# Softmax weights two steps closer to their maxima, and the maxima's transpose one step earlier

## The chip, the cores and the metric

The kernel runs on one core of a Trainium2 chip. The metric is the device time of one execution in microseconds (us). The time before is 3572.62 us, the median of 3 runs (3572.36 to 3573.77).

## The reference

One layer over 4096 tokens of width 256: attention with 16 heads of width 16, then a gated feed-forward network of width 1024, each with a residual and a layer norm.

```python
proj = quant4(x) @ ternary_weight(Wqkv_w).T + Wqkv_b      # q, k, v all from one projection
q = proj.reshape(B, N, h, dk).transpose(0, 2, 1, 3)
k = proj.reshape(B, h, N, dk);  v = proj.reshape(B, h, N, dk)
q, k = rotary(q, N), rotary(k, N)
ql, kl = q @ U, k @ U
att = einsum('bhnr,bhmr->bhnm', ql, kl) / sqrt(dk)
y = softmax(att, axis=-1) @ v
x = layernorm(x + quant4(y) @ ternary_weight(Wo_w).T)
h = silu(tlin(x, w1)) * tlin(x, w2);  h = gelu(tlin(h, h1));  h = gelu(tlin(h, h2))
x = layernorm(x + tlin(h, w3))
```

The softmax is the large part: 16 heads of 4096 by 4096 scores, each needing the maximum of its row before the exponential.

## The kernel before

**Units and steps.** Attention is cut into 64 units (`NU`). A unit is a pair of heads and a block of 512 queries; unit u has pair u // 8 and query block u % 8. A unit takes 32 steps (`NKT`), and one list of steps s runs through all units: step s belongs to unit s // 32. The order on every engine is the order in which this loop issues work; nothing rearranges it. Work other than the three streams below is put in a table `todo` with `at(step, f)`, and a step first runs its entries in the order in which they were put there:

```python
for s in range(NKT * NU + LAG + AVLAG + 4):
    while todo.get(s):
        todo[s].pop(0)()
    if s < NKT * NU and s % 2:
        largest(s)
    if 0 <= s - LAG < NKT * NU:
        weights(s - LAG)
    if s < NKT * NU and not s % 2:
        largest(s)
```

So an odd step has its table entries, then maxima, then weights; an even step has its entries, then weights, then maxima.

**Three streams.** `largest(s)` (L660, L671) makes scores with TensorE, 128 queries by 512 keys for each of the two heads, and VectorE reduces each to its maximum. In steps before `LAG` both heads' scores lie in one PSUM tile of the pool `ps_sc` and one reduction (L668) covers both. From then on they take two of the three single-bank buffers of `ps_1`. `weights(s - LAG)` (L709, L717) makes the scores again with the keys on the partitions: a first matmul subtracts the maxima (operand `m_rows`), a second adds the scores, ScalarE takes the exponential. `values` (L731), every second step and `AVLAG` = 4 steps behind the weights, multiplies them with v.

**The maxima's way.** At the last step of unit u VectorE folds the partial maxima into `m` (L676). One step after the unit's end, at 32 (u + 1) + 1, `largest_parts(u)` splits them into two float32r parts, the high one by ScalarE (L683), the low one by GpSimd (L684). Two steps later `largest_rows(u)` has VectorE transpose them into `m_turned` (L690), and the SyncE queue stores them to `m_dram` (L695) and, when that has landed, loads them twice as rows, one half for each head, into `m_rows` (L698). The unit's first `weights` step, 32 u + `LAG`, reads `m_rows`.

**What else hangs on `LAG`.** `end` = 32 u + `LAG` + 35 is the step of `finish(u)` (ScalarE copies the unit's result, L749). From it eight VectorE transposes `turn` (L763, at `end` + 2 to `end` + 16), the `gather` (four stores `y_raw`, L771, and a load `y`, L781, at `end` + 18), `add_strips` (GpSimd, L792, at `end` + 26) and `divide` (VectorE L801, GpSimd L803, a store L809, at `end` + 28).

**What does not.** In units 0 to 7 the projections of the eight token blocks run beside the attention, at fixed steps. For block b, counted from step 32 (b - 1): the queue's loads of `keys` (L545) at 28 for b of 3 and more, TensorE's product with them `times_g` (L553, with a VectorE subtraction L556) at 34 and 36, stores of `k_dram` (L592) at 37, and for the next block a scale round trip `ma_dram` (L469), `scale` (L471) and the table `cs_q` (L339) at -2. The keys `kT` of the next pair (L600, four loads of 512 KB) come at steps 40, 48, 56 and 64 from the start of the unit with query block 2. The first front of the feed-forward part, `integers` (L131 to L154 on VectorE), is put at step 2048 + 2, its transposes (L160) at 2048 + 8. The feed-forward stage follows the loop.

Of the kernel before, what the change touches and what calls it, by code (L numbers as in the profile page):

```python
# [27 lines left out]
NKT = N // P  # L28
# [9 lines left out]
def attn_ffn_kernel(  # L38
# [262 lines left out]
    with ExitStack() as actx:  # L301
# [295 lines left out]
        def load_keys(pair, kT, j, d):  # L597

            row = 64 * j + 32 * d
            nc.sync.dma_start(  # L600
                out=kT[row : row + 32].bitcast(F32),
                in_=k_dram[pair][j].rearrange("i e c n -> (i e) (c n)"),
            )

        def load_queries(u):

            pair, qb = divmod(u, NQB)
            qTs[u] = qpool.tile([P, QB], F32R, name="qT", bufs=3)
            for j in range(2):
                for i in range(2):  # L610
                    row = 64 * j + 2 * DK * i
                    nc.sync.dma_start(
                        out=qTs[u][row : row + 2 * DK, :].bitcast(F32),
                        in_=q_dram[qb][2 * pair + j, i].unsqueeze(0).broadcast_to([2, DK, QB]),
                    )
# [17 lines left out]
            project(held, sgn_qkv, bank1, i0, evacuate)  # L633

        NU = (H // 2) * NQB
        LAG = NKT + 8
        AVLAG = 4
        kTs, qTs, mxs, ms, avs, probs = {}, {}, {}, {}, {}, {}
        yas, yts, y4s, ys = {}, {}, {}, {}
# [2 lines left out]
        def at(step, f):  # L642
            todo.setdefault(step, []).append(f)

        def largest(s):
# [6 lines left out]

            both = ps_sc.tile([P, 2, QB], F32, name="sc") if s < LAG else None
            ps = [
# [26 lines left out]
        def largest_parts(u):  # L681
            parts, m = m_parts[:, 0], ms.pop(u)
            nc.scalar.copy(parts[:, :, 0, :], m)  # L683
            nc.gpsimd.tensor_tensor(  # L684
                parts[:, :, 1, :], m, parts[:, :, 0, :].bitcast(F32), ALU.subtract
            )

        def largest_rows(u):

            nc.vector.transpose(  # L690
                m_turned, m_parts.bitcast(F32).rearrange("p a j k t -> p (a j k t)")
            )

            rows = m_dram[u % 2]
            nc.sync.dma_start(out=rows.rearrange("r (b c) -> b r c", b=4), in_=m_turned)  # L695
            rows = rows[: 4 * BT].rearrange("(j k t) c -> j k (t c)", j=2, k=2)
            for j in range(2):
                nc.sync.dma_start(  # L698
                    out=m_rows[u % 2][64 * j : 64 * j + 2, :].bitcast(F32), in_=rows[j]
                )  # L700
# [19 lines left out]
        def values(s):  # L720

            u, kt = divmod(s, NKT)
            pair = u // NQB
            if kt == 0:
                avs[u] = ps_av.tile([P, QB], F32, name="av")
            for j in range(2):
                for k in range(2):
                    c, a = divmod(kt + k, 2)
                    strip = 32 * (2 * j + k)

                    nc.tensor.matmul(  # L731
                        avs[u][strip : strip + 32, :],
                        lhsT=v_all[
                            :, 2 * (2 * pair + j) + a, c * (DK + 1) : c * (DK + 1) + 32
                        ],
                        rhs=probs[s + k][:, j, :],
                        start=(kt == 0),
                        stop=(kt == NKT - 2),
                    )
            del probs[s], probs[s + 1]  # L740

        def finish(u):


            if u < NU - 1:
                yas[u] = qpool.tile([P, QB], F32, name="ya", bufs=1)
            else:
                yas[u] = last_unit[:, :QB]
            nc.scalar.copy(yas[u], avs.pop(u))  # L749
            if u < NU - 1:  # L750
                yts[u] = qpool.tile([P, QB], F32, name="yt", bufs=1)
# [8 lines left out]
        def turn(u, i):  # L760


            nc.vector.transpose(yts[u][:, ts(i, 64)], yas[u][:, ts(i, 64)])  # L763

        def gather(u):

            del yas[u]
            raw = y_raw[u % 2]
            yt = yts.pop(u).rearrange("p (b e) -> p b e", e=32)
            for strip in range(4):  # L770
                nc.sync.dma_start(  # L771
                    out=raw.rearrange("(b q) s e -> s q b e", q=32)[strip],
                    in_=yt[32 * strip : 32 * strip + 32],
                )
            if u < NU - 1:
                y4s[u] = qpool.tile([P, BT, 2, 2, 32], F32, name="y4", bufs=1)
            else:
                y4s[u] = last_unit[:, QB:].rearrange(
                    "p (t j k e) -> p t j k e", t=BT, j=2, k=2
                )  # L780
            nc.sync.dma_start(  # L781
                out=y4s[u].rearrange("p t j k e -> p t (j k e)"),
                in_=raw.rearrange("(t p) s e -> p t (s e)", p=P),
            )

        def add_strips(u):
            y4 = y4s.pop(u)
            if u < NU - 1:
                ys[u] = qpool.tile([P, BT, 2, DK + 1], F32, name="y", bufs=1)
            else:  # L790
                ys[u] = y4[:, :, :, 0, : DK + 1]
            nc.gpsimd.tensor_tensor(  # L792
                ys[u], y4[:, :, :, 0, : DK + 1], y4[:, :, :, 1, : DK + 1], ALU.add
            )

        def divide(u):

            pair, qb = divmod(u, NQB)
            y = ys.pop(u)
            den = stat.tile([P, BT, 2], F32, name="den")  # L800
            nc.vector.reciprocal(den, y[:, :, :, DK])  # L801
            yu = stat.tile([P, BT, 2, DK], F32, name="yu", bufs=2)
            nc.gpsimd.tensor_tensor(  # L803
                yu,
                y[:, :, :, :DK],
                den.unsqueeze(3).broadcast_to([P, BT, 2, DK]),
                ALU.mult,
            )
            nc.sync.dma_start(  # L809
                out=y_dram[qb].rearrange("(t p) d -> p t d", p=P)[  # L810
                    :, :, pair * 32 : (pair + 1) * 32
                ],
                in_=yu.rearrange("p t j e -> p t (j e)"),
            )
# [33 lines left out]
        with tc.manual_schedule():  # L848
# [85 lines left out]
            for u in range(NU):  # L934
                pair, qb = divmod(u, NQB)
                if qb == 2 and pair + 1 < H // 2:

                    def start_keys(pair=pair, u=u):
                        kTs[pair + 1] = kpool.tile([P, N], F32R, name="kT")
                        for i in range(4):  # L940
                            at(
                                NKT * u + 40 + 8 * i,
                                lambda i=i: load_keys(pair + 1, kTs[pair + 1], i // 2, i % 2),
                            )

                    at(NKT * u + 8, start_keys)
                if u:
                    at(NKT * (u - 1) + (25 if u < 3 else 23 if u < NQB else 14), lambda u=u: load_queries(u))
                base = NKT * u + LAG
                for kt in range(0, NKT, 2):  # L950
                    at(base + kt + 1 + AVLAG, lambda s=NKT * u + kt: values(s))
                at(NKT * (u + 1) + 1, lambda u=u: largest_parts(u))
                at(NKT * (u + 1) + 3, lambda u=u: largest_rows(u))
                end = base + NKT + AVLAG - 1
                at(end, lambda u=u: finish(u))
                if u == NU - 1:
                    left += [turn_last, lambda u=u: add_strips(u), lambda u=u: divide(u)]
                    continue
                for i in range(8):
                    at(end + 2 + 2 * i, lambda u=u, i=i: turn(u, i))  # L960
                at(end + 18, lambda u=u: gather(u))
                at(end + 26, lambda u=u: add_strips(u))
                at(end + 28, lambda u=u: divide(u))
# [33 lines left out]
            at(last - 60, start_front)  # L997
# [9 lines that stand above are left out]
# [259 lines left out]
```

## Time and profile before

| what | value |
|---|---|
| median of 3 runs | 3572.62 us |
| the profiled execution | 3571.62 us, span 3569.5 us |
| granted TensorE clock, mean | 0.994 |
| attention at full rate, unit 54 (2400.0 to 2443.2) | 43.20 us for 32 steps, PE busy 43.20, DVE 41.34, ACT 31.58 |
| maxima alone, ahead of the first weights (39 to 80 us) | DVE busy 38.04 of 41.00, PE 30.42 |
| weights and values alone, behind the last maxima (2855.4 to 2893 us) | PE busy 37.42 of 37.60, ACT 30.98, DVE 9.06 |
| chain that ended last | PE 97%, DVE 2%, DMA 1%, POOL 1% |
| DMA | mean 40 GB/s; q1, the SyncE queue's, 13.9% of 16 engines |

Times are microseconds from the start of the span of one profiled execution. PE is TensorE's matmuls, PEld its weight loads, DVE VectorE, ACT ScalarE, POOL GpSimd, SPq the SyncE queue that issues DMAs. Matmul ends are modelled, so a full PE row means that matmuls follow each other, and starts are what is to be read. A time behind a row in brackets is idle time of the engine before it, with what ended it.

### The profile page before, as it was taken

The numbers are of one execution on the slowest core, as the hardware profiler recorded it, in microseconds if no ns is written. First come the engines' busy times: TensorE is split into PE (matmuls) and PEld (weight loads), VectorE is DVE, ScalarE is ACT, GpSimd is POOL, SyncE is SP. The second block draws the span as 40 slices with busy tenths as digits, with TensorE's granted clock in tenths as the row PEclk, the third lists the DMA queues.
The fourth block names the chain that finished last, engine by engine and source line by source line (L and its number), as shares of the span: only waits on it lengthen the run. The fifth ranks groups of instructions, "written<-read, shape, count | busy, mean of one in ns | idle before, by whom it ended". The sixth has DMA issues, their size and how long they took to land.

```text
span 3569.5 us, 61116 instructions
## 1 busy us (share of the span) xinstructions
PE 3527.7 (99%) x23855; PEld 1983.6 (56%) x23855; DVE 3042.7 (85%) x5575; ACT 2337.1 (65%) x2713; POOL 437.1 (12%) x530
## 2 busy tenths in 40 slices
PE   6999999999999999999999999999999999999999
PEld 3444555555555555555555555555555458888887
DVE  8888999999999999999999999999999935555544
ACT  2677777777777777777777777777777753333333
POOL 5766200000000000000000000000000010000000
PEclk8999999999999999999999999999999999999999
DMA  3343212111211121111111111111121030000000
GB/s 102 89 121 89 55 27 50 27 27 30 51 29 27 27 50 27 28 37 42 27 27 44 33 27 27 44 27 24 47 68 33 24 93 1 25 30 18 18 7 13
DMA packets 267826, 141.88 MB, mean 40 GB/s; under 512 B 184584, under 2 KB 243848, under 8 KB 266632
## 3 DMA queue, kind: packets, MB, share of 16 engines
q1 hardware_dynamic: 263704, 126.35, 13.9%
q0 software_dynamic: 3824, 11.54, 1.0%
q8 instruction: 189, 3.10, 0.4%
q14 instruction: 109, 0.89, 0.1%
HBM read 91.57 MB, written 42.07 MB: 37 GB/s over the span
## 4 chain that ended last, share of the span: by engine, by line
PE 97%; DVE 2%; DMA 1%; POOL 1%; ACT 0%; issue 0%; SPq 0%; POOLq 0%; ACTq 0%
PE av L731 28%; PE sc L709 27%; PE ps L660 22%; PE ps_mm L1045 18%; DVE mx L668 1%; PE ps L553 1%; PE ps L483 0%; PE ps L172 0%; PE ps_mm L172 0%; PE ps_mm L290 0%; PE ps_mm L1087 0%; DMA qT<-q_dram 0%; DMA ma_dram<-ma_turned 0%; PE sc L660 0%; PE ps L160 0%
## 5 line engine op out<-in xcount | busy, mean ns | idle before, releaser
L671 DVE TENSOR_REDUCE mx<-ps 128x1 f32<-128x512 f32 x4016 | 2501.4, 683 | 137.4 <-PE ps L660 82.2
L717 ACT ACTIVATE pr<-sc 128x1024 f32<-128x1024 f32 x2048 | 1994.8, 1021 | 738.1 <-PE sc L709 736.4
L731 PE MATMUL av<-pr,v_all 128*32 128x512 f32 x8192 | 1092.1, 605 | 0.0
L660 PEld LDWEIGHTS ps<-kT,qT 64*128 64x128 f32 x4016 | 546.1, 183 | 949.7 <-DVE mx L671 812.0
L660 PE MATMUL ps<-kT,qT 64*128 64x512 f32 x4016 | 1015.4, 469 | 2.5 <-DMA qT<-q_dram 2.1
L709 PE MATMUL sc<-m_rows,minus 64*128 64x512 f32 x4096 | 823.1, 396 | 0.5 <-DVE mx L668 0.3
L709 PE MATMUL sc<-qT,kT 64*128 64x512 f32 x4096 | 815.5, 392 | 0.0
L709 PEld LDWEIGHTS sc<-m_rows,minus 64*128 64x128 f32 x4096 | 390.9, 185 | 95.0 <-ACT pr L717 36.4
L709 PEld LDWEIGHTS sc<-qT,kT 64*128 64x128 f32 x4096 | 390.6, 185 | 85.7
L731 PEld LDWEIGHTS av<-pr,v_all 128*32 128x32 f32 x8192 | 161.4, 108 | 257.4 <-issue 255.8
L1075 ACT ACTIVATE gate<-ps_mm,sc_hs 128x512 f32<-128x512 f32 x128 | 88.2, 689 | 288.5 <-PE ps_mm L1045 248.4
L283 DVE CAST h<-gate 128x512 fp32r<-128x512 f32 x128 | 54.3, 424 | 223.6 <-ACT gate L1075 223.4
L684 POOL TENSOR_TENSOR m_parts<-m,m_parts 128x8 fp32r<-128x8 f32 x64 | 13.0, 203 | 1809.6 <-ACT m_parts L683 1809.2
L285 DVE TENSOR_TENSOR h<-gate,h 128x512 fp32r<-128x512 f32 x192 | 132.3, 689 | 5.1
L1045 PE MATMUL ps_mm<-h,h1a 128*128 128x512 f32 x512 | 128.9, 394 | 0.0
L1067 DVE SCALAR_TENSOR_TENSOR gate<-ps_mm,sc_s,gate 128x512 f32<-128x512 f32 x64 | 47.9, 749 | 94.1 <-ACT gate L1065 73.9
L1045 PE MATMUL ps_mm<-h,h2a 128*128 128x512 f32 x512 | 127.1, 390 | 0.0
L1045 PE MATMUL ps_mm<-h,h1b 128*128 128x512 f32 x512 | 126.5, 389 | 0.0
L1045 PE MATMUL ps_mm<-h,h2b 128*128 128x512 f32 x512 | 126.5, 389 | 0.0
L763 DVE STREAM_TRANSPOSE yt<-ya 128x64 f32<-128x64 f32 x504 | 116.9, 233 | 0.0
L1045 PEld LDWEIGHTS ps_mm<-h,h1b 128*128 128x128 f32 x512 | 96.1, 188 | 20.1
L1045 PEld LDWEIGHTS ps_mm<-h,h2b 128*128 128x128 f32 x512 | 96.1, 188 | 19.9
(199 smaller groups left out, 1721.1 us busy)
## 6 DMA issues: line engine op xcount, KB each, us to landing
y_raw<-yt SPq DMA_DIRECT2D x256, 64.0 KB
qT<-q_dram SPq DMA_DIRECT2D x252, 64.0 KB
y<-y_raw SPq DMA_DIRECT2D x63, 256.0 KB
kT<-k_dram SPq DMA_DIRECT2D x28, 512.0 KB
xs<-in_x SPq DMA_DIRECT2D x16, 512.0 KB
q_dram<-qk SPq DMA_DIRECT2D x32, 256.0 KB
k_dram<-qk SPq DMA_DIRECT2D x56, 128.0 KB
cs_q<-in_csq SPq DMA_DIRECT2D x8, 512.0 KB
```

The costliest lines, as they stand in the source:

```text
L283: eng(dst[:, k, 0, :], g)
L285: nc.vector.tensor_tensor(dst[:, k, 1, :], g, dst[:, k, 0, :].bitcast(F32), ALU.subtract)
L553: nc.tensor.matmul(ps, lhsT=gmat, rhs=held["keys"][:, x], start=True, stop=True)
L660: nc.tensor.matmul(ps[j], lhsT=qTs[u][rows, ts(qt, P)], rhs=kTs[u // NQB][rows, ts(ck, 512)], start=True, stop=True,)
L671: nc.vector.tensor_reduce(mxs[u][:, qt, j, ck : ck + 1], ps[j], AX.X, ALU.max)
L709: nc.tensor.matmul(ps[:, j, :], lhsT=minus[rows, :] if first else kTs[u // NQB][rows, ts(kt, P)], rhs=m_rows[u % 2][rows, :] if first else ...
L717: nc.scalar.activation(pr, ps, AF.Exp)
L731: nc.tensor.matmul(avs[u][strip : strip + 32, :], lhsT=v_all[:, 2 * (2 * pair + j) + a, c * (DK + 1) : c * (DK + 1) + 32], rhs=probs[s + k ...
L763: nc.vector.transpose(yts[u][:, ts(i, 64)], yas[u][:, ts(i, 64)])
L1045: nc.tensor.matmul(ps, lhsT=sb[:, ks, ts(o, P)] if split else wo[:, k, :], rhs=src[:, k, i, :], start=(k == 0 and i == 0), stop=(k == n - ...
L1067: nc.vector.scalar_tensor_tensor(g, pb, scales["s2"][:, o : o + 1], gate, ALU.mult, ALU.mult)
L1075: nc.scalar.activation(g, ps, AF.Gelu, scale=scales[sc][:, o : o + 1])
```

## The change

`LAG` goes from 40 to 38: every weights and values step, and with them `finish`, the turns, the gather, the addition and the division, stand two steps earlier against the maxima; the loop has two steps fewer. `largest_rows` goes from three steps behind the unit's end to two, an even step instead of an odd one.

```diff
         NU = (H // 2) * NQB
-        LAG = NKT + 8
+        LAG = NKT + 6
         AVLAG = 4
...
                 at(NKT * (u + 1) + 1, lambda u=u: largest_parts(u))
-                at(NKT * (u + 1) + 3, lambda u=u: largest_rows(u))
+                at(NKT * (u + 1) + 2, lambda u=u: largest_rows(u))
                 end = base + NKT + AVLAG - 1
```

## Prediction

> **What bounds the kernel now.** I read the page's shares and its chain first, then the timeline of one boundary between units, then the SyncE queue around the early units, then the two ends of the attention. The page says that TensorE sets the time:
>
> ```profile
> PE 3527.7 (99%) x23855; PEld 1983.6 (56%) x23855; DVE 3042.7 (85%) x5575; ACT 2337.1 (65%) x2713; POOL 437.1 (12%) x530
> ...
> PE 97%; DVE 2%; DMA 1%; POOL 1%; ACT 0%; issue 0%; SPq 0%; POOLq 0%; ACTq 0%
> ```
>
> The timeline around the end of unit 21 shows one period of two steps and the way of the maxima:
>
> ```profile
> 1027.82 0.20 POOL L684 TENSOR_TENSOR m_parts<-m,m_parts 128x8 fp32r<-128x8 f32 x1 [34.67 <-ACT m_parts L683]
> ...
> 1029.06 1.06 PE L731 MATMUL av<-pr,v_all 128*32 128x512 f32 x8
> ...
> 1030.29 0.20 DVE L690 STREAM_TRANSPOSE m_turned<-m_parts 128x32 f32<-128x32 f32 x1
> ...
> 1030.52 0.57 SPq L695 DMA_DIRECT2D m_dram<-m_turned  x1
> ...
> 1031.76 1.07 PE L731 MATMUL av<-pr,v_all 128*32 128x512 f32 x8
> ...
> 1032.50 0.54 SPq L698 DMA_DIRECT2D m_rows<-m_dram  x2
> ...
> 1033.32 0.19 PEld L709 LDWEIGHTS sc<-m_rows,minus 64*128 64x128 f32 x2
> 1033.55 0.39 PE L709 MATMUL sc<-m_rows,minus 64*128 64x512 f32 x2
> ...
> 1036.26 0.40 PE L709 MATMUL sc<-m_rows,minus 64*128 64x512 f32 x2
> ```
>
> The values come at 1029.06 and again at 1031.76: 2.70 us for two steps, 43.20 for the 32 of a unit, with TensorE matmuls back to back. VectorE has four reductions in a period, 0.60 apart, so about 0.2 is free. The first matmul that reads unit 21's `m_rows` is the last row, at 1036.26. So in mid-kernel neither the place of the transpose nor the lag is on the path, as long as `m_rows` lands in time; what the change can give lies at the two ends, and what it can cost lies in the slack of that landing.
>
> **The two ends.** After the change two maxima steps fewer stand alone at the start, two weights steps fewer at the end, and two more are combined, with the same matmuls in all. At the start a step alone takes VectorE's L668 (four in 4.61 us from 79.12, and 1.17 apart in other rows): two are 2.34. The combined pair costs 2.70. Start: 2.70 - 2.34 = +0.36. At the end the values follow each other at 2865.31, 2867.42, 2869.78, 2871.91 and 2874.27, so a pair of steps takes 2.11 to 2.36: -2.24. In the last unit the weights wait for their rows, and the transpose stands behind the 5 us of `integers`:
>
> ```profile
> 2852.84 0.20 DVE L690 STREAM_TRANSPOSE m_turned<-m_parts 128x32 f32<-128x32 f32 x1
> ...
> 2856.52 0.77 PE L709 MATMUL sc<-m_rows,minus 64*128 64x512 f32 x2 [0.18 <-DMA m_rows<-m_dram]
> ```
>
> Both are now put at step 2050, and the transpose was put there first, so VectorE runs it ahead: it starts when POOL's L684 is done, near 2849.2, and the 0.18 goes. `integers` then waits for it, from 2847.84 to about 2849.4; its end moves from 2852.92 to 2854.5, under the transposes that need it (L160, 2855.72). Without that cover of 1.2 us the remainder would be lost on TensorE. Ends together: 0.36 - 2.24 - 0.18 = -2.06.
>
> **The landing in mid-kernel.** The weights come two steps earlier, 2.70 us; the first reader moves from 1036.26 to 1033.55, its weight load to 1033.32. The transpose passes only the last two reductions ahead of it, 2 x 0.60: from 1030.29 to 1029.09. L684 ended at 1028.02, so VectorE doesn't wait there; behind L690 on VectorE stand the reductions of one step. They start 0.20 later, as they do behind L676 (0.22, in the same kind of place at 1026.51), after which the next values still came in a period of 2.70: cost nothing. The trip from transpose to readable rows: the semaphore records have the second `m_rows` transfer landed at 1034.12, 3.83 after the transpose, and the last unit's pair of rows, 2852.84 to 2856.52 and a wait, agrees within 0.15. New landing 1029.09 + 3.83 = 1032.92, 0.40 before the weight load and 0.63 before the matmul; over units 8 to 62 the same sum leaves 0.25 to 0.42. I take no stall. Finish, turns and `divide` keep their odd steps, hence the free 0.2 us of a period; GpSimd's L792 and the store L809 come two steps earlier, behind the maxima's way as before. Unit 7 is tight by the same sum (second row landed 4.63 after the transpose, five small scale loads ahead of it): between 0 and 0.4, taken as 0, because these loads follow the gather and leave earlier too.
>
> Here the Trainium skill speaks against the change. Its page "DMA: Bandwidth & Descriptors", section "Anatomy of one DMA", gives each transfer a fixed cost of about 2.0 us (written for GpSimd's queue). The rows have 1.98 for the store (1030.52 to the next issue at 1032.50) and 1.33 for the second load (1032.79 to 1034.12). By the page's figure twice, an estimate, the rows land at 1033.6 and each unit loses about 0.3 us, 16 us in all.
>
> **The early units, where the queue order changes.** The gather moves from step 29 to step 27 of a unit, and in the windows of units 2 to 6 that puts it ahead of the `keys` loads (step 28). In four of these five this is covered: in unit 2 the keys would go out near 169.8 instead of 164.8 and are read at 177.43. Unit 3 has the large `kT` loads too:
>
> ```profile
> 213.18 0.41 SPq L600 DMA_DIRECT2D kT<-k_dram  x1
> 214.38 3.05 SPq L545 DMA_DIRECT2D keys<-rot  x4
> 218.50 5.29 SPq L771 DMA_DIRECT2D y_raw<-yt  x4
> 226.14 0.38 SPq L781 DMA_DIRECT2D y<-y_raw  x1
> ...
> 230.20 0.59 SPq L600 DMA_DIRECT2D kT<-k_dram  x1
> 230.85 0.58 SPq L695 DMA_DIRECT2D m_dram<-m_turned  x1
> 237.00 0.54 SPq L698 DMA_DIRECT2D m_rows<-m_dram  x2
> ```
>
> `kT` is not through before 223.4 by the semaphores, and the load `y` waits for the four stores behind it. With the gather first, `y` goes near 224.7, the keys at 225.1 to 227.5, the second landing near 227.8: `times_g`, at 227.03 before, waits about 0.8. The queue then reaches `m_dram` 0.76 later, 231.6, and as it needs 6.15 us behind `cs_q` and `kT`, the rows land at 238.61 + 0.76 = 239.4. Their reader, the matmul of 235.62, stands at 236.4 by then: a stall of 3.0. Unit 3 costs 3.8. The low bound is 0: the stores leave 2.7 earlier, and if `y` does too, the queue drains earlier and nothing waits. I take 3.8 because `kT`, not the turn, ended the stores' wait in this trace. Unit 1: GpSimd's L684 ends at 131.00, and the transpose would now stand at 130.22, so VectorE waits up to 0.8, with `times_g` on TensorE behind it. Bounds 0 and 0.8; I take 0.8.
>
> **Sum.** -2.06 + 3.8 + 0.8 = +2.5 on the profiled execution's 3571.62, so 3574.1; the median lies 1.0 above that execution: 3575.1.
>
> **Rivals.** (A) The sum above, 3575. (B) The queue drains in time in units 1 and 3: only the ends are left, 3572.6 - 2.1 = 3570.5. For it: everything that the gather issues is ready 2.7 earlier. (C) The rows come late in every unit. It decides from the point where the trip takes over 4.23 us (3.83 + 0.40). An excess of 0.3 over units 7 to 62 is 56 x 0.3 = 17: about 3592, the side of slower. For it: the margin is a tenth of the trip. Against it: 55 trips in this trace lie within 0.2 us of each other. (D) The stall in unit 3 halves the TensorE clock:
>
> ```profile
> 122.40:129.20 6.80, 6.45 (x19) 2.12 (x21) 1.98 (x3) 1.23 (x2) 6.46 (x8) 0.50 0.47 144
> ```
>
> In this stretch the granted clock is 0.50 for 6.80 us, after TensorE had waited for `qT` and buffers from 120.6 on; half of that, 3.4, would come on top of (A): 3578.5. The page "TensorE: Matmul & The Clock Gate", Part 1, has the clock halve after an idle window of about 3.4 us, so a stall of 3.0 is on its edge. Clock windows may fall otherwise around the first weights too (81.4 to 88.2 at 0.50): 1 us either way, in the range.
>
> **How the numbers follow.** A 0.50, B 0.30, D 0.10, C 0.08, 0.02 for what I don't see. A measurement of this kernel can tell about 0.2% (7.1 us) from no change. A and B lie inside it, D inside but near its edge (3579.8), C beyond. Faster 0.03, within 0.83, slower 0.14. The range 3569.5 to 3581 takes in A, B with its microsecond, and D; C is left out.
>
> **What would show it.** Right: period 2.70 and m_rows rows without a bracket in units 8 to 62; the `keys` rows behind the `y` row in unit 3, with a bracket "DMA" before L553 or L709 there; one pair less of values behind the last maxima; L690 ahead of L131 at 2849. Wrong: brackets "DMA m_rows" in many units (C), or unit 3 without any (B).

## The result, and the profile after

The changed kernel takes 3577.38 us (median of 22 runs, 3574.97 to 3580.48); the kernel before took 3572.07 in the runs beside it (22 runs, 3570.57 to 3573.93). The ratio is 1.0015, 95% interval 1.0009 to 1.0022: 5.3 us slower, inside the predicted range and within 0.2%. The profiled execution of the changed kernel took 3575.91 us with a span of 3573.7, against 3571.62 and 3569.5 before. A second profiled execution of each kernel, both on one chip, gave spans of 3574.3 and 3568.5.

The page's shares and its chain, after:

```profile
PE 3527.8 (99%) x23848; PEld 1986.6 (56%) x23855; DVE 3044.7 (85%) x5577; ACT 2336.8 (65%) x2713; POOL 436.6 (12%) x530
...
PE 94%; DVE 2%; POOL 2%; issue 1%; DMA 1%; ACT 0%; SPq 0%; POOLq 0%; ACTq 0%; DVEq 0%
```

TensorE still sets the time. The timeline of the changed kernel around the end of unit 21 answers to the one shown of before:

```profile
1031.79 0.20 POOL L684 TENSOR_TENSOR m_parts<-m,m_parts 128x8 fp32r<-128x8 f32 x1 [37.37 <-ACT m_parts L683]
...
1033.04 1.07 PE L731 MATMUL av<-pr,v_all 128*32 128x512 f32 x8
1033.07 0.20 DVE L690 STREAM_TRANSPOSE m_turned<-m_parts 128x32 f32<-128x32 f32 x1
...
1033.30 0.58 SPq L695 DMA_DIRECT2D m_dram<-m_turned  x1
...
1035.29 0.54 SPq L698 DMA_DIRECT2D m_rows<-m_dram  x2
...
1035.74 1.07 PE L731 MATMUL av<-pr,v_all 128*32 128x512 f32 x8
...
1037.31 0.19 PEld L709 LDWEIGHTS sc<-m_rows,minus 64*128 64x128 f32 x2
```

The values are 2.70 apart. The store takes 1.99 to the next issue. The second load of rows landed at 1037.04 by the semaphores, 3.97 after the transpose, and the weight load at 1037.31 has no bracket: the margin is 0.27 us. By the semaphores the margin lies between 0.18 and 0.42 in 52 of the units 8 to 62; units 29 and 61, with trips of 4.25 and 4.46, have none left. Of the units 7 to 62 only unit 56 waits.

To see where the 4 to 6 us are, I took the start of the values' matmuls (L731) at equal steps in both kernels; the difference after minus before, taken stretch by stretch, is the loss of that stretch. The last column is the second pair of executions. The loss of steps 269 to 1805, where it is spread over all units, is called the slow loss below.

| stretch | predicted | first pair | second pair |
|---|---|---|---|
| first weights and unit 1 (to step 77) | +1.16 | +0.94 | +1.17 |
| steps 77 to 109 | 0 | +0.09 | +0.12 |
| steps 109 to 141, with unit 3's first weights | +3.8 | +2.31 | +4.10 |
| steps 141 to 269 | 0 | +0.43 | +0.32 |
| steps 269 to 1805, most of the 43.2 us units | 0 | +1.18 | -0.19 |
| steps 1805 to 1837, with unit 56's first weights | 0 | +1.15 | +1.09 |
| steps 1837 to 2029 | 0 | +0.24 | +0.20 |
| steps 2029 to 2053, the last maxima | 0 | +0.82 | +0.83 |
| step 2053 to the last values | -2.42 | -2.61 | -2.54 |
| behind the last values | 0 | -0.39 | +0.68 |
| sum | +2.5 | +4.2 | +5.8 |

**Unit 1**, timeline of the changed kernel:

```profile
129.47 0.20 POOL L684 TENSOR_TENSOR m_parts<-m,m_parts 128x8 fp32r<-128x8 f32 x1
...
129.71 0.21 DVE L690 STREAM_TRANSPOSE m_turned<-m_parts 128x32 f32<-128x32 f32 x1 [1.95 <-POOL m_parts L684]
...
130.55 0.50 PE L660 MATMUL ps<-kT,qT 64*128 64x512 f32 x1 [1.82 <-DVE mx L671]
```

VectorE waits 1.95 us for GpSimd's low parts, and TensorE 1.82 behind it; in the second execution it is 3.60 and 3.47. From 119 to 132 us TensorE is idle for 2.15 and 1.96 us in the two executions of before, and for 3.48 and 3.59 in the two of the changed kernel.

**Unit 3**, timeline of the changed kernel:

```profile
224.19 0.38 SPq L781 DMA_DIRECT2D y<-y_raw  x1
...
224.66 2.46 SPq L545 DMA_DIRECT2D keys<-rot  x4
...
228.56 1.10 PE L553 MATMUL ps<-keys,gmat 128*128 128x512 f32 x2 [0.38 <-DMA keys<-rot]
...
230.49 0.60 SPq L600 DMA_DIRECT2D kT<-k_dram  x1
...
231.19 0.57 SPq L695 DMA_DIRECT2D m_dram<-m_turned  x1
...
237.13 0.54 SPq L698 DMA_DIRECT2D m_rows<-m_dram  x2
...
238.63 0.84 PE L709 MATMUL sc<-m_rows,minus 64*128 64x512 f32 x2 [1.35 <-DMA m_rows<-m_dram]
```

The `keys` now stand behind `y`, as predicted (225.1 to 227.5 there, 224.66 to 227.12 here), and the product with them waits. The store of the maxima goes out right behind a `kT` load of 512 KB and is through 5.94 us later; the weights wait 1.35 us for the rows.

**Unit 56**, timeline of the changed kernel:

```profile
2552.14 0.57 POOL L194 DMA_DIRECT2D w<-in_w2T  x1
...
2553.05 0.57 SPq L695 DMA_DIRECT2D m_dram<-m_turned  x1
...
2556.75 0.54 SPq L698 DMA_DIRECT2D m_rows<-m_dram  x2
...
2558.20 0.70 PE L709 MATMUL sc<-m_rows,minus 64*128 64x512 f32 x2 [0.77 <-DMA m_rows<-m_dram]
```

GpSimd issues a 512 KB load of feed-forward weights 0.9 us ahead of the store; the store takes 3.70 and not 1.99, and the margin is gone. Before, the load stood 2.5 us ahead of the store. Timeline of the kernel before:

```profile
2546.80 0.57 POOL L194 DMA_DIRECT2D w<-in_w2T  x1
...
2549.28 0.57 SPq L695 DMA_DIRECT2D m_dram<-m_turned  x1
...
2551.27 0.54 SPq L698 DMA_DIRECT2D m_rows<-m_dram  x2
```

**The last maxima**, timeline of the changed kernel:

```profile
2855.59 0.21 DVE L690 STREAM_TRANSPOSE m_turned<-m_parts 128x32 f32<-128x32 f32 x1 [1.32 <-POOL m_parts L684]
2855.72 1.18 DVE L131 TENSOR_REDUCE most<-yb 128x4 f32<-128x1024 f32 x1
...
2856.93 0.16 DVE L137 TENSOR_REDUCE ma<-most 128x4 f32<-128x8 f32 x1
...
2857.13 0.20 ACT L141 ACTIVATE ma<-ma 128x4 f32<-128x4 f32 x1 [0.72 <-DVE ma L137]
...
2858.30 0.50 PE L709 MATMUL sc<-m_rows,minus 64*128 64x512 f32 x2 [0.66 <-ACT pr L717]
```

The transpose runs ahead of `integers`, as predicted. But `integers` has an instruction on ScalarE, L141, between two exponentials. It waits 0.72 for VectorE, the next exponential waits behind it, and the weights wait 0.66 for that.

### The profile page after: what moved, and what is told of

It is laid out like the page before. It is cut to its first block, busy times and chain, and to the rows that moved or that the text cites. A ratio compares the mean times of both kernels' runs of the same rounds, so it can differ in the third digit from the quotient of the medians.

```text
span 3573.7 us, 61125 instructions
## 1 busy us (share of the span) xinstructions
PE 3527.8 (99%) x23848; PEld 1986.6 (56%) x23855; DVE 3044.7 (85%) x5577; ACT 2336.8 (65%) x2713; POOL 436.6 (12%) x530
## 4 chain that ended last, share of the span: by engine, by line
PE 94%; DVE 2%; POOL 2%; issue 1%; DMA 1%; ACT 0%; SPq 0%; POOLq 0%; ACTq 0%; DVEq 0%
PE av L731 27%; PE sc L709 26%; PE ps L660 21%; PE ps_mm L1045 18%; DVE mx L668 1%; PE ps L553 1%; DVE mx L671 0%; DMA m_dram<-m_turned 0%; PE ps L483 0%; PE ps_mm L172 0%; PE ps_mm L290 0%; PE ps_mm L1087 0%; PE ps L172 0%; ACT pr L717 0%; PE ps L580 0%
## 5 line engine op out<-in xcount | busy, mean ns | idle before, releaser
L731 PE MATMUL av<-pr,v_all 128*32 128x512 f32 x8192 | 1091.9, 605 | 0.1
L731 PEld LDWEIGHTS av<-pr,v_all 128*32 128x32 f32 x8192 | 161.8, 108 | 258.0 <-issue 256.0
L684 POOL TENSOR_TENSOR m_parts<-m,m_parts 128x8 fp32r<-128x8 f32 x64 | 12.9, 202 | 1961.9 <-ACT m_parts L683 1961.5
```

Source lines behind the costliest of these rows:

```text
L731: nc.tensor.matmul(avs[u][strip : strip + 32, :], lhsT=v_all[:, 2 * (2 * pair + j) + a, c * (DK + 1) : c * (DK + 1) + 32], rhs=probs[s + k ...
```

## The experiments

Theory: the changed kernel's 2.5 us and more are rows that come late where something large lies on the queue or the DMA engines, plus waits at the two ends. Rivals: the order of gather and keys alone (unit 3), late landings by chance (unit 56), and a loss in every unit from the transpose's new place.

**The lag alone.**

```diff
 # against the kernel before
-        LAG = NKT + 8
+        LAG = NKT + 6
```

> The weights 38 steps behind, the transpose left three steps behind the fold. Theory (the maxima's way is on the path as soon as its 3.83 us from transpose to landed rows is not over at the first weight load): the trace of before has the second half of unit 21's rows landed at 1034.12 and the load would stand at 1033.32, so each of the units 7 to 62 stalls by about 0.8 us with a bracket 'DMA m_rows' at its first weights; 56 x 0.8 = 45, time about 3617 to 3623. Rival (the landing is not what the weights wait for, other slack in the two steps takes it up): no brackets, about 3577, as with both edits.

3618.17 us against 3572.81 (ratio 1.0125, 1.0106 to 1.0143), +45.4. Timeline of this kernel, unit 21:

```profile
1044.38 0.20 DVE L690 STREAM_TRANSPOSE m_turned<-m_parts 128x32 f32<-128x32 f32 x1
...
1044.61 0.58 SPq L695 DMA_DIRECT2D m_dram<-m_turned  x1
...
1046.60 0.54 SPq L698 DMA_DIRECT2D m_rows<-m_dram  x2
...
1048.21 0.67 PE L709 MATMUL sc<-m_rows,minus 64*128 64x512 f32 x2 [0.40 <-DMA m_rows<-m_dram]
```

The trip is the same, the reader stands 3.83 behind the transpose and waits. From step 269 to 2029 this kernel loses 37.5 us in 55 units, 0.68 each (0.8 expected). The margin was read rightly: without the second edit the first one costs 45 us.

**The transpose alone.**

```diff
 # against the kernel before
-                at(NKT * (u + 1) + 3, lambda u=u: largest_rows(u))
+                at(NKT * (u + 1) + 2, lambda u=u: largest_rows(u))
```

> The transpose two steps behind the fold, the weights still 40 behind. Theory (the extra time of the changed kernel all comes from the lag; the moved transpose costs VectorE nothing): within 1 us of before, 3571 to 3573, no drift in the periods of units 7 to 62, no stall at the rows. Rival (the transpose in an even step delays the reductions behind it a little in each unit): the same slow loss as with both edits, 0.02 to 0.03 us in each of 56 units, so 3573.3 to 3574, with single periods of 2.705 to 2.708 at the start of units.

3576.76 us against 3572.81, ratio 1.0008 (0.9999 to 1.0017). The theory of this run falls, and the median lies over the rival's 3573.3 to 3574 too: moved alone, the transpose takes about 4 us, though the interval just reaches no change. At equal steps against the first profile of before it loses 1.73 by step 77, where this execution has 17.0 us of half clock from 79 us on and that one 13.6, 0.1 in each of the next units (4.11 us for a period that had 4.02), 2.00 from step 269 to 1805, 0.83 at the last maxima, and gains 0.24 behind them. Here the end of the prediction is seen apart: of the changed kernel's -2.6 behind step 2053 only 0.24 are the transpose's.

**The gather back at its step.**

```diff
 # against the changed kernel
-                at(end + 18, lambda u=u: gather(u))
+                at(end + 20, lambda u=u: gather(u))
```

> The changed kernel with the gather 20 steps behind the unit's end and not 18, so that it stands again at the same step as before, behind the loads of keys in the early units. Theory (unit 3 loses its time to the rows, which wait in the SyncE queue behind a 512 KB load of kT whatever the order of gather and keys; the rows are read 2.7 us earlier than before and land no earlier): the wait at the product with the keys goes, the wait at unit 3's first weights grows to about 2.4 us by so much, and the time stays at 3576.5 to 3577.5. Rival (the order of gather and keys is the cause, as the prediction had it): unit 3 loses under 0.5 us, time about 3575.

3579.14 us against 3572.81, ratio 1.0017 (1.0008 to 1.0026): no gain, and more than the 3576.5 to 3577.5 of the theory. Timeline of this kernel, unit 3:

```profile
229.85 0.59 SPq L600 DMA_DIRECT2D kT<-k_dram  x1
...
230.48 0.58 SPq L695 DMA_DIRECT2D m_dram<-m_turned  x1
...
236.60 0.54 SPq L698 DMA_DIRECT2D m_rows<-m_dram  x2
...
238.15 0.76 PE L709 MATMUL sc<-m_rows,minus 64*128 64x512 f32 x2 [2.31 <-DMA m_rows<-m_dram]
```

The wait at the product with the keys is gone, and the wait for the rows is longer: 2.31 where the changed kernel had 1.35. Unit 3 costs 4.28, part of it a stretch of half clock (below). So the order of gather and keys, on which the prediction had put the loss, only sets at which of two places TensorE waits; what ends it is the store behind `kT`.

**The two weight loads earlier.**

```diff
 # against the changed kernel
-                at(last - 230 + 10 * k, lambda k=k: load_w2(k))
+                at(last - 232 + 4 * k, lambda k=k: load_w2(k))
```

> The changed kernel with GpSimd's two weight loads of the feed-forward part at steps 1816 and 1820 and not 1818 and 1828, so that the second is queued ahead of the low parts of unit 56 and not right behind them. Theory (the 512 KB of that load lie on the DMA engines while unit 56's maxima are stored, 3.70 us in place of 1.98, and the rows come late): no bracket at the rows of unit 56, 1.1 us less than the changed kernel, 3576.3. Rival (the late landing was chance and can fall in any unit): the time stays at 3577.4, and other units show such a stall.

3576.22 us against 3572.81, ratio 1.0011 (1.0002 to 1.0020): 3.4 over before where the changed kernel had 5.3, a step as large as expected or larger, but the intervals overlap. The timeline of this kernel in unit 56 decides it; the loads went out together, 38 us ahead of the store:

```profile
2518.09 1.11 POOL L194 DMA_DIRECT2D w<-in_w2T  x2
...
2556.09 0.57 SPq L695 DMA_DIRECT2D m_dram<-m_turned  x1
...
2558.08 0.54 SPq L698 DMA_DIRECT2D m_rows<-m_dram  x2
```

1.99 for the store, no bracket, a loss of 0.08 in place of 1.15. The stall in unit 56 is the load's. In the runs with the loads in their old place and the rows as late (the gather back, and the next one) it stood in unit 56 again, 1.00 and 0.80.

**The gather back and `kT` later.**

```diff
 # against the changed kernel
-                at(end + 18, lambda u=u: gather(u))
+                at(end + 20, lambda u=u: gather(u))
...
-                                NKT * u + 40 + 8 * i,
+                                NKT * u + (40 if pair else 44) + 8 * i,
```

> The changed kernel with the gather 20 steps behind the unit's end, and the four kT loads of the first pair each four steps later (the last at step 132, behind the store and load of unit 3's maxima, not at step 128 ahead of them). Theory (with the gather back, unit 3 loses 2.3 to 4.3 us only because its 16 KB store waits 6.1 us behind the 512 KB load): the store lands about 2 us after its issue, no bracket at unit 3's first weights, unit 3 costs under 0.5 us, time 2.3 to 4.3 less than with the gather alone put back, about 3574 to 3576 beside a kernel before of 3572.5. Rival (cs_q ahead of them delays the store as much): the trip stays over 4 us and the stall at 2 us or more, time 3578 to 3579.

3575.14 us against 3572.96, ratio 1.0005 (0.9996 to 1.0014). Timeline of this kernel, unit 3:

```profile
230.68 0.57 SPq L695 DMA_DIRECT2D m_dram<-m_turned  x1
...
233.90 0.56 SPq L698 DMA_DIRECT2D m_rows<-m_dram  x2
...
234.50 0.31 SPq L600 DMA_DIRECT2D kT<-k_dram  x1
```

With `kT` behind the rows, the store takes 3.22, nothing waits, and unit 3 loses 0.12. `cs_q`, 512 KB as well and still ahead, accounts for at most what is left over 1.99; the store takes 3.03 to 3.70 in the three later kernels that keep `kT` behind the rows and the lag at 38.

**All three repairs.**

```diff
 # against the kernel with the gather back and kT later
-                at(last - 230 + 10 * k, lambda k=k: load_w2(k))
+                at(last - 232 + 4 * k, lambda k=k: load_w2(k))
```

> As the kernel with the gather back and the kT loads later, and GpSimd's two weight loads at steps 1816 and 1820 too. Theory: the parts add, unit 3 under 0.5 us and unit 56 under 0.1, so 1.1 us less than that kernel: about 3573 to 3575; what is left over the kernel before is the drift of the moved transpose, 0.03 to 0.04 us in each of 56 units. Rival (late landings only move to other units): no less than that kernel.

3573.74 us against 3572.96, ratio 1.0002 (0.9993 to 1.0011), 1.4 less than the kernel ahead of it in the same comparison. Unit 3 loses 0.09 and unit 56 0.08: the parts add.

**The transpose later.**

```diff
 # against the kernel before
-                at(NKT * (u + 1) + 3, lambda u=u: largest_rows(u))
+                at(NKT * (u + 1) + 4, lambda u=u: largest_rows(u))
```

> The kernel before with the transpose four steps behind the fold, an even step as in the change, but two steps farther from the fold; the weights 40 behind. Rows land at about 1031.6 + 3.8 = 1035.4 in unit 21, 0.6 ahead of their weight load. Theory (the drift comes from the fold's 0.22 us and the transpose's 0.20 falling on VectorE within two periods that have 0.2 us free each): units 8 to 62 drift under 0.01 us each, time within 1 us of before, 3572 to 3573.5. Rival (an even step itself is the bad place, the transpose standing between the reductions of one period): the same 0.04 us in each unit as with the transpose at two steps, and about 1 us at the last unit less: 3575 to 3577.

3576.51 us against 3572.96, ratio 1.0008 (0.9999 to 1.0017). The theory would have had 3572 to 3573.5. In this execution steps 269 to 1805 lose 2.12, as much as with the transpose two steps behind the fold. This spoke for the rival, until the next runs.

**Lag 39, the transpose left at three.**

```diff
 # against the kernel before; the kT loads later, as above
-        LAG = NKT + 8
+        LAG = NKT + 7
...
-                end = base + NKT + AVLAG - 1
+                end = base + NKT + AVLAG
...
-                if s < NKT * NU and s % 2:
+                if s < NKT * NU and not s % 2:
                     largest(s)
...
-                if s < NKT * NU and not s % 2:
+                if s < NKT * NU and s % 2:
                     largest(s)
```

> Weights 39 steps behind, the transpose left three behind the fold; values, finish and gather keep their steps against the weights or the maxima as far as parity allows (maxima and weights change places in odd and even steps), and the first pair's kT loads four steps later. Theory (half the gain of the ends, rows 0.5 us ahead of their load, no drift since the transpose is three steps behind the fold): tail 1.1 less, head 0.2 more, no stalls in units 3 and 7 to 62: 0.5 to 1.5 us faster than before, 3571 to 3572. Rival (the swapped order costs VectorE or TensorE something in every period): slower, by 0.02 us in each of 1000 periods 20 us, about 3592.

3626.37 us against 3572.96, ratio 1.0149 (1.0133 to 1.0164). Neither theory nor rival: timeline of this kernel, end of unit 20's values.

```profile
1056.91 0.58 ACT L749 COPY ya<-av 128x512 f32<-128x512 f32 x1
...
1057.54 0.16 PEld L731 LDWEIGHTS av<-pr,v_all 128*32 128x32 f32 x8 [1.15 <-ACT ya L749]
```

In this kernel `finish` keeps its old odd step, so it stands one step ahead of the next unit's values and not two, and the values wait for it: 0.6 to 1.0 in nearly every unit. The lag of 39 itself is neither confirmed nor refuted; none of the units 7 to 62 waited for rows.

**Both kernels once more.**

> The kernel before, unchanged, in a second profiled execution, to see how far two executions of one kernel differ at equal steps. Theory (the slow loss of 2.4 us over units 8 to 62 belongs to the moved transpose): this execution stands within 0.5 us of the first profile at each unit, apart from a shift of up to 1 us made at the first weights. Rival (the slow loss is a condition of the execution, which any kernel can meet): it loses 1 us or more against the first profile between units 8 and 62.

> The changed kernel, unchanged, in a second profiled execution. Theory: unit 56 stalls by 1.0 to 1.2 us again and unit 3 costs 2.3 to 4.3 us, since both come from the order of the queues; the last unit's step behind the maxima costs 0.83 again. Rival (late landings by chance): one of the stalls is missing or stands in another unit.

3570.63 and 3576.46 us. Unit 56 stalls again (1.10), the last maxima cost 0.82 again: not chance. Unit 3 costs 4.1 this time. The slow loss does not come back: from step 269 to 1805 the second execution of the changed kernel is 0.09 faster than the first profile of before, and the second of before 0.10 slower. With the same middle part but for the gather's step, the slow loss was 1.18, 0.68, 1.97, 0.61, 1.98 and 0.27 us in the first execution of the changed kernel and in five kernels made from it. So it can come and go with nothing changed, and no single profile can put it on the code; both theories about the transpose's place, that of its distance from the fold and that of the even step, are without their ground. The kernel before shifts by more than that from one comparison to the next: its medians were 3572.81, 3572.96 and 3570.23. Why some executions have the loss, and whether the moved transpose makes it more frequent, stays open: neither of the two profiles of before has it.

Unit 3 cost 2.31 in one execution and 4.1 to 4.3 in four others. The windows of the changed kernel from 240 to 243 us ("PEclk" is the granted clock), first and second execution:

```profile
core 0: us, PE busy (x) PEld busy (x) DVE busy (x) ACT busy (x) POOL busy (x), PEclk, DMA share, GB/s
240.00:243.00 3.00, 2.86 (x21) 1.20 (x17) 2.35 (x4) 1.90 (x3) 0.00 (x0) 1.00 0.51 161
```

```profile
240.00:243.00 3.00, 3.00 (x15) 1.01 (x14) 1.51 (x3) 0.95 (x1) 0.00 (x0) 0.50 0.51 164
```

The second one has half clock for some 3.4 us behind its stall (0.97 in the microsecond from 239, 0.50 in the next three, 0.82 in the one from 243). The idle bracket of the rows was 1.35 in the first, without a halving, and 1.52, 1.60, 1.71 and 2.31 in the four executions with one. (In the two of 1.52 and 1.60 the view names ScalarE's L162, which ended within 0.12 us of the matmul's start; but in all five the matmul starts 0.13 to 0.14 us after the first load of rows landed by the semaphores.) In the nine other executions nothing waits for rows there, and the clock is 1.00 from 226 to 254 us. This is the prediction's rival D, on top of A, in four of the five executions that wait.

**The front one step later.**

```diff
 # against the kernel with all three repairs
-                for i, f in zip((0, 6, 10, 12, 16, 18, 20), steps):
+                for i, f in zip((1, 6, 10, 12, 16, 18, 20), steps):
```

> The kernel with gather back, kT loads later and the two weight loads earlier, and also the first part of the first front (integers) one step later, 2051, the rest of the front left. Theory (in the changed kernel VectorE holds integers back until GpSimd's low parts are done, 1.32 us; ScalarE's L141, queued between two exponentials, waits for it 0.72 us, and the weights wait for ScalarE): the bracket 'ACT pr' at the last weights of unit 62 goes and the time is 0.5 to 0.8 us less than without this edit, about 3573 beside a kernel before of 3572.9. Rival (the wait only moves to the transposes of the front): no less.

3571.05 us against 3570.23, ratio 1.0002 (0.9993 to 1.0011). Timeline of this kernel:

```profile
2850.92 0.21 DVE L690 STREAM_TRANSPOSE m_turned<-m_parts 128x32 f32<-128x32 f32 x1 [1.32 <-POOL m_parts L684]
...
2852.27 0.16 DVE L137 TENSOR_REDUCE ma<-most 128x4 f32<-128x8 f32 x1
...
2852.54 0.21 ACT L141 ACTIVATE ma<-ma 128x4 f32<-128x4 f32 x1
```

VectorE waits 1.32 as before, but L141 finds its operand ready. Steps 2029 to 2053 go from +0.85, in the kernel with all three repairs, to -0.09, while behind step 2053 the gain shrinks from -2.60 to -2.36: 0.7 us net. The mechanism at the last maxima is shown; the medians can't tell 0.7 us (+0.8 over before here and +0.8 without the edit, each in its own comparison). By its profile this is the best of the changed kernels, with its last values 0.78 ahead of the first profile of before and its span equal to the second one's (3568.5). It does not beat the kernel before.

**The transpose one step behind the fold.**

```diff
 # against the kernel with the front later
-                at(NKT * (u + 1) + 2, lambda u=u: largest_rows(u))
+                at(NKT * (u + 1) + 1, lambda u=u: largest_rows(u))
```

> As the kernel with integers one step later, with the transpose only one step behind the fold, the same step as the split into parts. Theory (an even step is the bad place for the transpose, as two and four steps behind the fold both showed it): the slow loss in units 8 to 62 goes down from 2.4 to under 0.5 us, as VectorE waits only 0.1 to 0.2 for GpSimd there; rows land 1.2 earlier; time 3570.5 to 3572, faster than the kernel before by about 1 to 2. Rival (VectorE waits for GpSimd's low parts in every unit, and its 0.2 us free in a period don't cover 0.35): a loss of 0.1 us or more in each unit, 3578 and over.

3583.49 us against 3570.23, ratio 1.0038 (1.0024 to 1.0051): the rival. Timeline of this kernel, unit 21:

```profile
1031.01 0.22 DVE L676 TENSOR_REDUCE m<-mx 128x8 f32<-128x64 f32 x1
...
1032.33 0.20 POOL L684 TENSOR_TENSOR m_parts<-m,m_parts 128x8 fp32r<-128x8 f32 x1 [37.40 <-ACT m_parts L683]
...
1032.56 0.21 DVE L690 STREAM_TRANSPOSE m_turned<-m_parts 128x32 f32<-128x32 f32 x1
...
1033.40 0.18 PEld L660 LDWEIGHTS ps<-kT,qT 64*128 64x128 f32 x1 [0.32 <-DVE mx L671]
```

The transpose starts 0.03 behind GpSimd's end: VectorE has waited 0.13, as in nearly every unit (7.6 us ahead of 61 transposes; the other three wait 8.6, most of it in unit 1), and the maxima's weights wait for its late reductions. Each unit from 7 to 55 loses 0.1 to 0.3. Of the places tried, two steps behind the fold is the earliest without this loss.

## Why the prediction was right, and where its steps were not

**The middle.** "I take no stall" held in 55 of 56 units: period 2.70, no bracket, margin 0.27 in unit 21 where 0.40 was worked out. Rival C did not come. It decides from a trip of 4.23, and the lag alone shows that the edge is about where it was put: each unit lost 0.68 where 0.8 was worked out. The Trainium skill's page "DMA: Bandwidth & Descriptors", section "Anatomy of one DMA", has a fixed 2.0 us for a transfer, written for GpSimd's queue; the store on SyncE's queue took 1.99, which agrees. The second load took 1.46 in unit 21 of the changed kernel, so the loss of 16 us that was estimated from the page did not come.

The step that failed here is the reading of the margin as one number for all units. It was taken from 55 trips of before, where the weight load of unit 56 went out at 2546.80, 2.5 us ahead of the store and not 0.9, and the store still took 1.99. Moving the transpose earlier moved the store into the load, and with 0.3 us left that is enough: 1.1 us.

**The early units.** The queue's order came as foretold. The sum of head and unit 1, +1.16, was measured as +0.94 and +1.17, but that agreement is luck. Unit 1's term was mis-sized: its upper bound of 0.8 took the end of GpSimd's L684 from one trace, and VectorE waited 1.95 and 3.60 for it (2.44 even in the second execution of before), with 1.3 to 1.6 us more idle time on TensorE than before. From 79 us to step 77 both executions of before have 13.6 us of half clock and both of the changed kernel 10.2, which works the other way by up to 1.7 us, and the two executions of before alone differ by 0.4 us at step 77. By step 45 the first pair already had +0.98, where the head's term was 0.36. Rival B, a queue that drains in time, did not come: unit 3 waits. Unit 3's term was 3.8: 0.8 at the keys and 3.0 at the rows. In the first pair the period of the keys lost 0.43 and that of the rows 1.74. The 3.0 set the reader at 236.4 and forgot the 1.0 that the units ahead had lost by then; the `kT` load ahead of the rows went out only 0.29 later than before (230.49 against 230.20). In the other executions the half clock brings the cost to 4.1 and more, so that the 3.8 lies between the two. That the cause was the gather passing the keys was wrong: the run with the gather back shows the same loss. The cause was in the sum as well, a reader 2.7 earlier behind a queue that moves no earlier, and that part is what was right.

The moved transpose was costed at nothing. In steps 141 to 269 it costs 0.1 a unit, 4.11 for a period of 4.02; the kernels with the transpose two or four steps behind the fold have it (at four steps in the period after that one), the lag alone and the second execution of before do not.

**The end.** The -2.42 that was worked out for the end stands behind the last maxima: -2.61 and -2.54 were measured. But "`integers` then waits, under the transposes that need it" named only VectorE and TensorE; ScalarE's L141 is part of `integers`, and the exponentials queue behind it. That is +0.83 at the last maxima, shown by taking it away; the net gain of that is 0.7, as 0.24 less is gained behind step 2053.

**The clock.** Rival D had 0.10, as an alternative to A at 3578.5. Its mechanism came in four of the five profiled executions that wait in unit 3, at about half its price: 3.4 us of half clock and not 6.8, and 1.8 to 2.0 us on top of the 2.31 without it. How many of the 22 runs have it is not known; their median lies between A and D. The page "TensorE: Matmul & The Clock Gate", Part 1, speaks of free-running windows of some 3.4 us and of an idle window of that length; the halved stretch behind unit 3 has that length, but the runs show it after brackets of 1.52 to 2.31 us.

The terms that were missed (unit 56 1.1, the last maxima 0.8, 0.4 in the early units) add up to 2.3, as much as lies between the 3575.1 of the sum and the median. That the rest cancels is luck: unit 1, unit 3's clock and the slow loss go to either side from one execution to the next. With the three repairs and the later front the change is worth nothing measurable.

What is not settled: the kernels with the transpose alone, two and four steps behind the fold, have medians 3.95 and 3.55 over before, and their profiles account for about 3.3 and 1.0 once the slow loss is left out.

## What to carry to other kernels

A margin read from quiet units holds for quiet units: before it is spent, look in every unit for the large transfers of all queues that pass near it, and price the few that will meet. When a wait is added on one engine, follow every instruction of the delayed group, on each engine that has one, to what is queued behind it. And where a reader moves earlier while its data stand in a queue that other transfers hold, the loss is the move itself, whatever the order of the small transfers ahead.

## What the runs showed of the hardware

A load of 512 KB on GpSimd's queue, issued 0.9 us ahead, stretched a 16 KB store on SyncE's queue from 1.99 to 3.70 us. One of 512 KB (`kT`) some 0.7 us ahead on the same queue stretched it to 5.94 to 6.26, with `cs_q` ahead as well. In all nine executions with `kT` ahead, the store of unit 3's maxima was through 6.6 to 7.0 us after the issue of `kT`, whether it went out 0.6 us behind it or 3.4 (the transpose later, 3.37 for the store). The time goes by the large load's issue, not by the store's.

The half clock falls at other places in other executions of one kernel. Windows of the second execution of before:

```profile
122.40:129.20 6.80, 6.80 (x40) 2.48 (x32) 3.76 (x6) 3.64 (x6) 6.38 (x8) 1.00 0.36 121
131.80:135.20 3.40, 3.40 (x15) 1.03 (x15) 1.88 (x4) 0.00 (x0) 0.00 (x0) 0.50 0.16 40
```

The first had 0.50 from 122.40 to 129.20; here it is full clock there and half clock for 3.4 us from 131.8. Between steps 45 and 77 these two executions of the same code differ by 1.1 us, about the size of the predicted terms of head and unit 1 together.

Over 1500 steps with the same code, executions differ by up to 2.1 us (the second of the changed kernel and the one with the weight loads earlier, on one chip). The loss comes as more periods of 2.702 to 2.711 us beside those of 2.700, at all places of a unit: 527 of 768 periods are of 2.700 in the one and 165 in the other. A drift in one profile is no evidence about an edit until a second profile shows it.
